# Routing 4096 tokens in three groups of 8, 12 and 12 tiles in place of two of 16

## The chip, the cores and the metric

The kernel runs on one core of one Trainium2 chip. The metric is the device time of one execution in microseconds (us), the median of several runs. The core has five engines with a queue of instructions each: TensorE (PE, with its weight loads as PEld), VectorE (DVE), ScalarE (ACT), GpSimd (POOL) and SyncE (SP). They wait for each other through semaphores; 16 DMA engines move data.

## What is computed

A mixture-of-experts layer with 8 experts, top 2, behind a rotation of the features:

```python
x_rotated = hamilton(q_left_n, hamilton(x_filtered, q_right_conj))   # L0_cond: a fixed map of the 512 features
logits = xf @ gate_w.T                                               # xf: 4096 tokens x 512
scores = softmax(logits); topv, topi = top_k(scores, 2)
gates = topv / sum(topv)
for j in range(2):                                                   # place of each token within its expert
    mask = one_hot(topi[:, j], 8)
    loc_in = cumsum(mask, axis=0) - 1 + offset
    locs.append(loc_in at topi[:, j]); offset = offset + mask.sum(axis=0)
valid = loc < 1024                                                   # capacity
disp[topi * 1024 + loc] += xf * valid
h = relu(disp @ fc1_w.T + fc1_b); eo = h @ fc2_w + fc2_b             # per expert: 1024 x 512 -> 2048 -> 512
out = x + sum over the two choices of eo[topi * 1024 + loc] * gates * valid
```

The rotation is linear in the features and the same for all tokens, so the kernel folds it into a 4x4 matrix `M` per lane and into the gate's weights.

## The kernel before

**Three stages.** First a routing stage, inside `with ExitStack() as rctx` (L166 to L535): it works out, for each of the 8 x 1024 slots, which token fills it (`slot_tok`), and from that the indices for the later gathers and scatters. Then the expert stage (L704 to L1017): TensorE multiplies the gathered tokens with 32 blocks of weights, in a form of Strassen's algorithm with seven products where the plain form has eight (L715, L728), while the other engines gather the next expert's rows, rotate them and add up results. Scatters write the rows back. The order of all instructions is written out by hand: both stages run under `tc.manual_schedule()`, so each engine has its instructions in the order in which the program names them.

**Routing.** The 4096 tokens are 32 tiles of 128, taken in two groups of `TG` = 16 tiles. For each group:

- SP loads four pieces of the transposed input, `xb[g, j]`, 1 MB each (L182). All eight stand at the head of SP's queue, and four loads of weights, 1 MB each, behind them (L107, L113). From the seventh on, a load waits for one that stands eight loads ahead of it, so several are always in flight.
- `logits` (L324): TensorE multiplies each piece with the folded gate weights `Gw`, 8 experts in 32 columns, four column strips side by side.
- `turned` (L338): VectorE transposes the sums from PSUM in 32x32 squares, so that tokens lie on partitions.
- `choose` (L344): VectorE finds the best and second best expert: eleven steps over `TG` x 8 elements, with one `exp` on ScalarE (L357) between them. Its result is wanted by the step at L365. Then a running sum over the tiles of the group in four steps with doubling distance (L371, L373), in bf16 tiles `cnt`, and a carry into the next group's (L377).
- `rank` (L383): two matmuls, with a triangular matrix and with ones, give each token's place within its expert.
- `places` (L395): six VectorE steps split the place into a tile number `hi` and a lane number `lo`.
- `one_hots` (L418): for 8 tiles (`TC`) at a time, VectorE compares `hi` and `lo` with tables of all tile numbers (`tile_no`) and all lanes (`lane`), in fp16: `B` (L428), `W` = `B` times the token's number (L429), and `A` (L433). The last chunk's `A` is made in two parts.
- `tokens` (L440): TensorE multiplies `A` with `W`, 16 small matmuls for each chunk, all into one PSUM tile, `tok_ps`, in which each slot then finds its token.

The order of these calls is the list at L454 to L496: group 0 up to its choice; half of group 1's logits; rank 0; the other half; places 0, the first chunk of one-hots and its tokens; group 1's choice, the totals (L467) and rank 1; group 0's second chunk; then places, both chunks and tokens of group 1. Between them POOL derives from the totals which slots are filled (L484 to L490). The tables `lane` and `tile_no` are made before all this by VectorE (L283 to L296) from counters that POOL writes (L205).

**What follows.** VectorE turns `tok_ps` into `slot_tok` (L501 to L504), after which POOL sends eight gathers of 128 rows (L560). TensorE transposes the first four (L680), VectorE and ScalarE rotate them (L690, L688), and the first matmuls of the expert stage start (L826). VectorE's other outputs of the stage (L505 to L535) are made beside that.

Of the kernel before, what the change touches and what calls it, by code (L numbers as in the profile page):

```python
# [37 lines left out]
P = 128  # L38
# [17 lines left out]

CW = 32
# [7 lines left out]
def kernel(  # L65
# [93 lines left out]
    TG = 16  # L159
    GROUPS = NT // TG  # L160
    TC = 8
# [4 lines left out]
    with ExitStack() as rctx:  # L166
# [12 lines left out]
        for g in range(GROUPS):  # L179
            for j in range(NJ):  # L180
                xb[g, j] = xp.tile([P, QT, TG * CW], F32, tag="xb", name=f"xb{g}_{j}")
                nc.sync.dma_start(xb[g, j], xt[g, j])  # L182
# [20 lines left out]
        def iota(shape, pattern, base, mult, name):  # L203
# [9 lines left out]
            iota([P, P], [[1, P]], 0, 0, "lane0"),  # L213
            iota([P, P], [[-1, P]], P - 1, 0, "lane1"),
# [9 lines left out]
        PAD = 8  # L224
        cnt = [
            [rp.tile([P, PAD + TG + 1, KE], BF16, name=f"cnt{g}_{i}") for i in range(5)]
            for g in range(GROUPS)
        ]
        for g in range(GROUPS):
            for i in range(4):  # L230
                nc.gpsimd.memset(cnt[g][i][:, :PAD], 0.0)

# [46 lines left out]
        lane = rp.tile([P, P, TC, K], F16, name="lane")  # L279
        tile_no = rp.tile([P, E, PT, TC, K], F16, name="tile_no")  # L280
        for k in range(K):
            lane_f = rp.tile([P, P], F32, name=f"lane_f{k}")
            V.tensor_copy(lane_f, lane_i[k])  # L283
            V.tensor_scalar(
                lane[:, :, :, k],
                lane_f.unsqueeze(2).to_broadcast([P, P, TC]),
                -mid,
                None,
                ALU.add,
            )  # L290
            tile_f = rp.tile(TILES, F32, name=f"tile_f{k}")
            V.tensor_copy(tile_f, tile_i[k])
            V.tensor_copy(
                tile_no[:, :, :, :, k].rearrange("p e s t -> p (e s) t"),
                tile_f.rearrange("p e s -> p (e s)").unsqueeze(2).to_broadcast([P, NS, TC]),
            )  # L296
        tile_no = tile_no.rearrange("p e s t k -> p (e s) (t k)")
# [16 lines left out]

        T8 = [P, TG, E]
        revb = rev.unsqueeze(1).to_broadcast(T8)
# [4 lines left out]

        lt_ps = [bank(rps, "lt", g) for g in range(GROUPS)]

        def logits(g, js):  # L324

            for j in js:
                for c in range(QT):
                    nc.tensor.matmul(
                        lt_ps[g][c * CW : (c + 1) * CW],
# [8 lines left out]
        def turned(g):  # L338

            t = gp.tile([P, TG, CW], F32, tag="lt", name=f"lts{g}")  # L340
            V.transpose(t.rearrange("p t w -> p (t w)"), lt_ps[g])
            lg[g] = t[:, :, :E]

        def choose(g):  # L344

            ts = slice(g * TG, (g + 1) * TG)
            mask = cnt[g][0][:, PAD : PAD + TG].rearrange("p t (k e) -> p t k e", k=K)
# [4 lines left out]
            mx = gp.tile([P, TG], F32, tag="mx", name=f"mx{g}")  # L352
            V.tensor_reduce(mx, lg[g], AX.X, ALU.max)
            d = gp.tile(T8, F32, tag="d", name=f"d{g}")
            V.tensor_tensor(d, lg[g], over_e(mx), ALU.subtract)
            ex = gp.tile(T8, F32, tag="ex", name=f"ex{g}")
            nc.scalar.activation(ex, d, AF.Exp)  # L357
            q = gp.tile(T8, F32, tag="q", name=f"q{g}")
            V.scalar_tensor_tensor(q, d, 0.0, revb, ALU.is_equal, ALU.mult)
            for k in range(K):  # L360
# [3 lines left out]
                if k == 0:  # L364
                    V.scalar_tensor_tensor(ex, mask[:, :, 0, :], -2.0, ex, ALU.mult, ALU.add)  # L365
                    V.tensor_reduce(second[:, ts], ex, AX.X, ALU.max)
                    q = gp.tile(T8, F32, tag="q", name=f"q1{g}")
# [4 lines left out]
            for i in range(1, 4):  # L372
# [3 lines left out]
            if g + 1 < GROUPS:  # L376
                V.tensor_tensor(  # L377
                    cnt[g + 1][0][:, PAD - 1], c[4][:, PAD + TG], c[0][:, PAD - 1], ALU.add
                )
# [3 lines left out]
        def rank(g):  # L383
            flat = bank(rps, "rank", g)[:, : TG * KE]
            rank_ps[g] = flat.rearrange("p (t c) -> p t c", c=KE)
            for n, (w, c) in enumerate(((upper, cnt[g][0]), (ones, cnt[g][4]))):
# [3 lines left out]
                    rhs=c[:, PAD : PAD + TG].rearrange("p t c -> p (t c)"),  # L390
                    start=n == 0,
                    stop=n == 1,
                )

        def places(g):  # L395


            each = [P, TG, K]
            r = gp.tile([P, TG, KE], F32, tag="r", name=f"r{g}")
            V.scalar_tensor_tensor(  # L400
                r, rank_ps[g], mid, cnt[g][0][:, PAD : PAD + TG], ALU.subtract, ALU.mult
            )
            loc = gp.tile(each, F32, tag="loc", name=f"loc{g}")
            V.tensor_reduce(loc, r.rearrange("p t (k e) -> p t k e", k=K), AX.X, ALU.add)
            h = gp.tile(each, F32, tag="h", name=f"h{g}")
            V.tensor_scalar(h, loc, 1.0 / P, BIG, ALU.mult, ALU.add)
            V.tensor_scalar(h, h, BIG, None, ALU.subtract)
            lo = gp.tile(each, F16, tag="lo", name=f"lo{g}")
            hi = gp.tile(each, F16, tag="hi", name=f"hi{g}")
            V.scalar_tensor_tensor(  # L410
                hi, rank_first[:, g * TG : (g + 1) * TG], -WIDE, h, ALU.mult, ALU.add
# [6 lines left out]
        def one_hots(g, c, hi, lo, parts=1):  # L418

            hi, lo = (  # L420
                a[:, c * TC : (c + 1) * TC].rearrange("p t k -> p (t k)") for a in (hi, lo)
            )
            tok = tok_no[:, g * TG + c * TC : g * TG + (c + 1) * TC].rearrange("p t k -> p (t k)")
            of_tile = [P, NS, TC * K]
            B = oh.tile(of_tile, F16, tag="B", name=f"B{g}_{c}")
            W[g, c] = oh.tile(of_tile, F16, tag="W", name=f"W{g}_{c}")
            A[g, c] = oh.tile([P, P, TC * K], F16, tag="A", name=f"A{g}_{c}")
            V.tensor_tensor(B, tile_no, hi.unsqueeze(1).to_broadcast(of_tile), ALU.is_equal)  # L428
            V.tensor_tensor(W[g, c], B, tok.unsqueeze(1).to_broadcast(of_tile), ALU.mult)  # L429
# [633 lines left out]
```

## Time and profile before

| what | us |
|---|---|
| median of 3 runs | 1633.86 (1632.6 to 1635.38) |
| the profiled execution | 1635.45 |
| its span | 1633.7 |
| busy: PE / DVE / POOL / ACT | 1584.2 / 922.1 / 893.0 / 283.1 |
| first group's last logits matmul ends | 15.83 |
| VectorE starts group 0 / group 1 (L341) | 15.85 / 26.74 |
| last token matmul ends | 43.53 |
| first row gather starts (L560) | 44.55 |
| first expert matmul starts (L826) | 56.29 |

Times within the execution are counted from the span's start. A line of the timeline or of the chain has a start, a length, the engine, and what it did; "x32" is a number of instructions. A group has a count, the sum of its busy time, the mean of one in ns, and what ended the idle time before it. A line such as L433 is one of the kernel before; after the change, lines lie some 8 to 40 further down.

### The profile page before, as it was taken

What the parts mean: (1) busy time and instruction counts of PE and PEld (TensorE: products, weight loads), DVE (VectorE), ACT (ScalarE), POOL (GpSimd) and SP (SyncE); (2) the same over time, 40 slices, a digit from 0 to 9 for tenths busy, and PEclk for the clock granted to TensorE, in tenths of its full rate; (3) what the DMA queues carried; (4) which work ended last, traced back from release to release, by engine and by line L of the source; (5) the groups of instructions that cost most, each with busy time, mean ns of one, the idle gap of its engine ahead of it and who ended that gap; (6) DMA issues with size and microseconds to landing.
All of it is one profiled execution on the core that took longest, in us unless ns stands there. A gap on an engine that the chain in (4) does not pass through costs nothing.

```text
span 1633.7 us, 14503 instructions
## 1 busy us (share of the span) xinstructions
PE 1584.2 (97%) x5558; PEld 1039.0 (64%) x5558; DVE 922.1 (56%) x1291; ACT 283.1 (17%) x393; POOL 893.0 (55%) x747
## 2 busy tenths in 40 slices
PE   4899999999999999999999999999999999999996
PEld 1456666666666666666666666666666666666665
DVE  7536744476555755567455774447745476454335
ACT  1121211221112211122111221122111221111110
POOL 1576265853568435783367726586266844544304
PEclk8799999999999999999999999999999999999999
DMA  7542103311222112320133210331122211230003
GB/s 311 172 152 72 52 31 113 114 60 52 97 97 72 52 52 110 124 82 1 52 137 108 72 52 7 137 111 63 52 97 75 89 52 52 104 108 31 21 26 102
DMA packets 47998, 137.31 MB, mean 84 GB/s; under 512 B 9334, under 2 KB 9590, under 8 KB 42808
## 3 DMA queue, kind: packets, MB, share of 16 engines
q1 hardware_dynamic: 22800, 75.54, 12.6%
q0 software_dynamic: 20736, 52.32, 9.7%
q10 hardware_dynamic: 4392, 8.52, 1.4%
q8 instruction: 44, 0.72, 0.2%
q14 instruction: 26, 0.21, 0.0%
HBM read 119.77 MB, written 25.23 MB: 89 GB/s over the span
## 4 chain that ended last, share of the span: by engine, by line
PE 93%; issue 2%; DVE 1%; DMA 1%; POOL 1%; ACT 1%; SPq 0%; POOLq 0%; another core or an unknown queue 0%; DVEq 0%; ACTq 0%
PE a L728 26%; PE a L715 26%; PE b L715 20%; PE b L728 19%; PE p L826 2%; DMA xb<-in_xt_dram 1%; POOL rows L560 1%; POOL out_dram L606 0%; DMA rows<-out_dram,slot_tok 0%; PE tok_ps L444 0%; ACT u L759 0%; DMA rows<-in_x_dram,slot_tok 0%; DVE A L433 0%; ACT h L789 0%; PE xps L680 0%
## 5 line engine op out<-in xcount | busy, mean ns | idle before, releaser
L759 ACT ACTIVATE u<-a,b_sb 128x512 f32<-128x512 f32 x186 | 127.7, 686 | 802.4 <-PE a L715 719.2
L637 POOL DMA_INDIRECT xq<-in_xq_dram,quarter x224 | 228.5, 1020 | 62.0 <-issue 60.2
L728 PEld LDWEIGHTS a<-t,hs 128*128 128x128 f32 x1024 | 194.6, 190 | 79.4 <-issue 59.3
L728 PE MATMUL a<-t,hs 128*128 128x256 f32 x1024 | 241.9, 379 | 0.0
L715 PE MATMUL a<-x,s 128*128 128x512 f32 x496 | 233.1, 592 | 0.0
L136 POOL TENSOR_TENSOR s<-w 128x512 f32<-128x512 f32 x31 | 39.3, 1268 | 228.9 <-PE b L715 228.8
L139 POOL TENSOR_TENSOR s<-w,s 128x512 f32<-128x512 f32 x31 | 40.3, 1299 | 202.6 <-PE b L715 202.5
L715 PEld LDWEIGHTS a<-x,s 128*128 128x128 f32 x496 | 94.2, 190 | 65.7 <-issue 59.3
L715 PE MATMUL a<-x,w 128*128 128x512 f32 x248 | 118.4, 600 | 8.1 <-ACT u L759 3.7
L728 PEld LDWEIGHTS b<-w,h 128*128 128x128 f32 x512 | 98.0, 192 | 43.0 <-issue 20.6
L728 PE MATMUL b<-w,h 128*128 128x256 f32 x512 | 122.0, 381 | 2.1 <-DVE acc L989 2.1
L728 PEld LDWEIGHTS a<-t,h 128*128 128x128 f32 x512 | 97.1, 190 | 40.5 <-issue 25.6
L728 PEld LDWEIGHTS a<-w,h 128*128 128x128 f32 x512 | 97.3, 190 | 39.7 <-issue 29.4
L728 PEld LDWEIGHTS b<-t,hs 128*128 128x128 f32 x512 | 97.3, 190 | 39.7 <-issue 25.3
L728 PEld LDWEIGHTS b<-w,hs 128*128 128x128 f32 x512 | 97.3, 190 | 39.2 <-issue 28.9
L728 PE MATMUL a<-t,h 128*128 128x256 f32 x512 | 121.1, 379 | 0.8 <-DVE v L976 0.8
L728 PE MATMUL a<-w,h 128*128 128x256 f32 x512 | 121.0, 379 | 0.0
L728 PE MATMUL b<-t,hs 128*128 128x256 f32 x512 | 120.9, 379 | 0.0
L728 PE MATMUL b<-w,hs 128*128 128x256 f32 x512 | 120.9, 379 | 0.0
L715 PE MATMUL a<-xa,w 128*128 128x512 f32 x248 | 116.6, 592 | 0.8 <-ACT u L759 0.8
L715 PE MATMUL b<-x,s 128*128 128x512 f32 x248 | 116.5, 592 | 0.0
L715 PE MATMUL b<-xb,s 128*128 128x512 f32 x248 | 116.5, 592 | 0.0
(169 smaller groups left out, 2154.0 us busy)
## 6 DMA issues: line engine op xcount, KB each, us to landing
w<-in_w_dram SPq DMA_DIRECT2D x64, 1024.0 KB, 7.8
xb<-in_xt_dram SPq DMA_DIRECT2D x8, 1024.0 KB, 8.6
out_dram<-in_x_dram ACTq DMA_DIRECT2D x1, 8192.0 KB
xq<-in_xq_dram,quarter POOLq DMA_INDIRECT x224
b<-in_b_dram POOLq DMA_DIRECT2D x8, 256.0 KB
c<-choice,slot_cho POOLq DMA_INDIRECT x64
rows<-out_dram,slot_tok POOLq DMA_INDIRECT x64
out_dram<-rows,slot_add POOLq DMA_INDIRECT x64
```

The lines of the kernel that those rows point to most:

```text
L136: lambda: G.tensor_tensor(s[0], w[:, 1, 0], w[:, 1, 1], ALU.add),
L139: lambda: G.tensor_tensor(s[3], w[:, 0, 1], s[1], ALU.subtract),
L560: nc.gpsimd.indirect_dma_start(out=t, out_offset=None, in_=src, in_offset=bass.IndirectOffsetOnAxis(ap=slot_tok[:, s : s + 1], axis=0),)
L637: nc.gpsimd.indirect_dma_start(out=self.xg[half][st][:, q * P : (q + 1) * P], out_offset=None, in_=xq, in_offset=bass.IndirectOffsetOnAxis ...
L715: nc.tensor.matmul(out[:, m], lhsT=factors[0][n][:, c, m * P : (m + 1) * P], rhs=factors[1][n][:, c, :], start=first and c == 0, stop=c == ...
L728: nc.tensor.matmul(out[:, m], lhsT=factors[0][n][:, c, (st0 + m) * P : (st0 + m + 1) * P], rhs=factors[1][n][:, c, :], start=first and m = ...
L759: nc.scalar.activation(to[:, m], a[:, m], func, bias=bias[:, m : m + 1])
L826: nc.tensor.matmul(ps[n][:, m], lhsT=w[:, block, i // 2, i % 2, m * P : (m + 1) * P], rhs=x.of(half, i), start=i == 0, stop=i == NJ - 1,)
```

## The change

- `TG` = 16 and `TC` = 8 give way to `GROUP = (8, 12, 12)`: three groups of different sizes. Twelve loads of `xt` (four of 0.5 MB, eight of 0.75 MB) take the place of eight of 1 MB. Tiles are made for 12 (`TM`) and cut to the group's size, so that group 0's pieces land in rows of 384 elements of which 256 are filled.
- One-hots are made for a whole group at once: three sets in place of four, the last with `A` in three parts.
- The tables `lane` and `tile_no` grow from 8 to 12 tiles and are written by ScalarE: `lane` ahead of group 0's `exp` on its queue, `tile_no` behind it. The lane counters are made twice as large with the middle already taken off, and ScalarE halves them.
- Group 0 needs three running-sum steps (`SUMS`), the others four. After 12 tiles the 16 long sum already covers the carried row, so the carry and the totals are then a copy and one matmul (`all_before`).
- The order of the calls is a new list, for three groups.

The rest of `choose`, `rank`, `places` and `tokens` changes only in sizes and names.

```diff
+GROUP = (8, 12, 12)
...
-    TG = 16
-    GROUPS = NT // TG
-    TC = 8
+    GROUPS = len(GROUP)
+    FROM = [sum(GROUP[:g]) for g in range(GROUPS)]
+    TM = max(GROUP)
...
-                xb[g, j] = xp.tile([P, QT, TG * CW], F32, tag="xb", name=f"xb{g}_{j}")
-                nc.sync.dma_start(xb[g, j], xt[g, j])
+                size = QT * GROUP[g] * CW
+                at = P * (NJ * QT * CW * FROM[g] + j * size)
+                xb[g, j] = xp.tile([P, QT, TM * CW], F32, tag="xb", name=f"xb{g}_{j}")[
+                    :, :, : GROUP[g] * CW
+                ]
+                nc.sync.dma_start(
+                    xb[g, j],
+                    xt[at : at + P * size].rearrange("(p c f) -> p c f", p=P, c=QT),
+                )
...
+        SUMS = [(n - 1).bit_length() for n in GROUP]
...
             V.tensor_copy(lane_f, lane_i[k])
-            V.tensor_scalar(
+            nc.scalar.activation(
                 lane[:, :, :, k],
-                lane_f.unsqueeze(2).to_broadcast([P, P, TC]),
-                -mid,
-                None,
-                ALU.add,
-            )
-            tile_f = rp.tile(TILES, F32, name=f"tile_f{k}")
-            V.tensor_copy(tile_f, tile_i[k])
-            V.tensor_copy(
-                tile_no[:, :, :, :, k].rearrange("p e s t -> p (e s) t"),
-                tile_f.rearrange("p e s -> p (e s)").unsqueeze(2).to_broadcast([P, NS, TC]),
-            )
+                lane_f.unsqueeze(2).to_broadcast([P, P, TM]),
+                AF.Copy,
+                scale=0.5,
+            )
+            tile_f.append(rp.tile([P, NS], F32, name=f"tile_f{k}"))
+            V.tensor_copy(tile_f[k], tile_i[k].rearrange("p e s -> p (e s)"))
+
+        def tile_tables():
+            for k in range(K):
+                nc.scalar.copy(
+                    tile_no[:, :, k::K], tile_f[k].unsqueeze(2).to_broadcast([P, NS, TM])
+                )
...
-            for i in range(1, 4):
+            for i in range(1, SUMS[g]):
                 V.tensor_tensor(
                     c[i + 1][:, PAD:], c[i][:, PAD:], c[i][:, PAD - 2**i : -(2**i)], ALU.add
                 )
             if g + 1 < GROUPS:
-                V.tensor_tensor(
-                    cnt[g + 1][0][:, PAD - 1], c[4][:, PAD + TG], c[0][:, PAD - 1], ALU.add
-                )
+                carry = cnt[g + 1][0][:, PAD - 1]
+                if len(all_before(g)) == 1:
+                    V.tensor_copy(carry, all_before(g)[0])
+                else:
+                    V.tensor_tensor(carry, *all_before(g), ALU.add)
+
+        def all_before(g):
+            n = GROUP[g]
+            own, before = cnt[g][SUMS[g]][:, PAD + n], cnt[g][0][:, PAD - 1]
+            return [own] if 2 ** SUMS[g] > n else [own, before]
...
-        def one_hots(g, c, hi, lo, parts=1):
+        def one_hots(g, hi, lo, parts=1):
+            hi, lo = (a.rearrange("p t k -> p (t k)") for a in (hi, lo))
+            n = GROUP[g] * K
...
+            B = oh.tile([P, NS, TM * K], F16, tag="B", name=f"B{g}")[:, :, :n]
+            W[g] = oh.tile([P, NS, TM * K], F16, tag="W", name=f"W{g}")[:, :, :n]
+            A[g] = oh.tile([P, P, TM * K], F16, tag="A", name=f"A{g}")[:, :, :n]
...
         logits(0, range(NJ))
         turned(0)
         choose(0)
-        logits(last, range(NJ // 2))
+        tile_tables()
+        logits(1, range(HJ))
         rank(0)
-        logits(last, range(NJ // 2, NJ))
+        logits(1, range(HJ, NJ))
         at = places(0)
-        one_hots(0, 0, *at)
-        tokens(0, 0)
-        turned(last)
-        choose(last)
+        one_hots(0, *at)
+        turned(1)
+        choose(1)
+        logits(2, range(HJ))
+        tokens(0)
+        rank(1)
+        logits(2, range(HJ, NJ))
+        at = places(1)
+        turned(2)
+        choose(2)
         tot_ps = bank(rps, "rank", NT)[:, :KE]
...
-        rank(last)
-        one_hots(0, 1, *at)
-        tokens(0, 1)
+        rank(2)
+        one_hots(1, *at)
+        tokens(1)
...
         at = places(last)
-        one_hots(last, 0, *at)
-        tokens(last, 0)
-        one_hots(last, 1, *at, parts=2)
-        tokens(last, 1)
+        one_hots(last, *at, parts=3)
+        tokens(last)
```

## The prediction

> **What bounds the kernel now.** I read the page first, then the chain of work that ended last.
>
> ```profile
> span 1633.7 us, 14503 instructions
> PE 1584.2 (97%) x5558; PEld 1039.0 (64%) x5558; DVE 922.1 (56%) x1291; ACT 283.1 (17%) x393; POOL 893.0 (55%) x747
> ```
>
> TensorE is busy 97% of the span, and the diff touches none of that work: only the routing before it. The order of instructions of the built kernel says so too: from the first row gather on, every engine has the same instructions as before. So the change can move only the moment at which `slot_tok` (L504) lets the gathers start; all that follows moves along. The start of the chain:
>
> ```profile
> 2.59 11.65 DMA xb<-in_xt_dram
> 14.28 1.54 PE lt L328 x8
> 15.85 0.73 DVE lts L341
> ...
> 38.15 1.14 DVE A L433
> 39.30 0.05 issue
> 39.34 4.20 PE tok_ps L444 x32
> ...
> 44.55 1.25 POOL rows L560
> ...
> 56.29 12.18 PE p L826 x24
> ```
>
> Three links (start, length, what): the first four 1 MB loads up to 15.85 (their matmuls end there), VectorE without a break to 39.30, 32 small matmuls to 43.55. Call the first moment T0. At most 44 us, 2.7% of the span, are in play. The durations that I scale, from the groups with shapes kept apart (count | busy us, mean ns):
>
> ```profile
> L433 DVE TENSOR_TENSOR A<-lane,lo 128x2048 f16<-128x2048 f16 x3 | 3.7, 1229 | 0.0
> L428 DVE TENSOR_TENSOR B<-tile_no,hi 128x1024 f16<-128x1024 f16 x4 | 2.7, 684 | 0.0
> L433 DVE TENSOR_TENSOR A<-lane,lo 128x1024 f16<-128x1024 f16 x2 | 1.3, 685 | 0.0
> L404 DVE TENSOR_REDUCE loc<-r 128x32 f32<-128x256 f32 x2 | 0.8, 420 | 0.1
> L359 DVE SCALAR_TENSOR_TENSOR q<-d,rev 128x128 f32<-128x128 f32 x2 | 0.6, 294 | 0.1
> ```
>
> 16-bit work: (1229-684)/1024 = 0.53 ns per element; fp32: (420-294)/128 = 1.0, I take 1.04; the rest, some 0.15 us, is paid per instruction whatever the size. The third row, parts of 8 out of 16 neighbours, costs no more than whole rows (second row), so I price group 0's rows (16 out of 24) the same.
>
> **T0, the first group.** It shrinks from 4 MB to 2 MB. Before, TensorE's waits for loads ended at 6.88, 9.29, 11.80, 14.28: 2.5 us per MB. Two MB would have landed at 9.3. But group 0 now goes into a tile of 12: 1 KB runs in place of 8 KB. The DMA view in windows has the nearest rows; the first is of 8 KB runs, the second is nearly all `w2`, with 2 KB runs:
>
> ```profile
> DMA packets 1107, 8.02 MB, mean 422 GB/s; under 512 B 128, under 2 KB 128, under 8 KB 128
> DMA packets 372, 0.80 MB, mean 401 GB/s; under 512 B 7, under 2 KB 7, under 8 KB 363
> ```
>
> A 2 KB run takes 82 to 86 ns of one of 16 engines (401 and 383 GB/s, two windows) where 422 GB/s makes it 78: 4 to 8 ns per run. A 1 KB run is then 39+7 = 46 ns, and 128 runs per engine cost 0.9 us more (bounds: 0, and 1.1). Against that, loads of half the size should land with less lead between engines, -0.4. So 9.3+0.9-0.4 = 9.8; the last four matmul pairs at half width take 1.0 (1.93 halved) and T0 = 10.85. Bounds 9.5 (no run cost, fast clock) and 11.4. That is 5.0 us earlier than 15.85.
>
> A rule speaks against smaller loads: the Trainium skill, "DMA: Bandwidth & Descriptors", section "Bandwidth", wants at least 1 MiB per DMA for 75% of peak, and gives 2.0 us + bytes/436e3 for each. By it, taken one after the other, four loads of 0.5 MB are 12.8 us. The trace's 1 MB loads, which the rule puts at 4.4, land every 2.5, as several are in flight; twelve loads keep that. I take the row.
>
> **VectorE's chain.** Group 0: before 15.85 to 26.82 = 10.97. With 8 tiles: transpose -0.27, eleven choice steps of 64 elements less -0.73, one of four running sums gone -0.40 and three halved -0.20, `r` and `loc` -0.27, small steps and rank -0.17; B, W, A keep their size. 8.93.
> Group 1 up to `hi`/`lo`: before 26.82 to 32.63 (transpose, choice, sums) 5.81 and 35.19 to 36.83 (places) 1.64. For 12 tiles -0.64 and -0.16. Its places now come at once after its sums, so they pay the trip to the rank matmul, 0.44 in group 0 (22.25 to 22.69). 7.09, at T0+16.0.
> Group 2's choice and sums: 5.17. Then B, W, A of group 1: before 2.56, B and W +0.27 each, A +0.54: 3.64. Places of group 2: 1.48. B and W of group 2: before 1.32, +0.54: 1.86. First third of A: 0.65.
> Sum: T0+16.0+5.17+3.64+1.48+1.86+0.65 = T0+28.8, plus a wait w.
>
> The wait: group 2's transpose needs its last two logits chunks, and TensorE's queue holds them behind `tokens(0)` and `rank(1)`, which waits for group 1's sums at T0+14.1 = 24.95. Rank 0.45, then two chunks of 384 columns: 0.8 each at the fast clock, 1.45 at the slow one (1.06 and 1.93 of the before trace at 512): ready at 26.9 to 28.2. VectorE asks at 26.85. w = 0.1 to 1.4; I take 0.7, since the clock before read 0.50 up to 25.6. Data are no later: the last MB landed at 24.3, +0.5 to 0.9. `tokens(0)` (16 matmuls, 2.19) stand behind group 2's first two chunks, which land at about 21, so they end at 24.2, just clear of 24.95.
>
> **The tail on TensorE.** Before, 32 token matmuls run after 39.34; now 24 after the first third of A. Two windows of 1 us (PE busy and count first, near the end the granted clock):
>
> ```profile
> 27.00:28.00 1.00, 1.00 (x9) 1.00 (x10) 0.93 (x3) 0.00 (x0) 0.00 (x0) 1.00 1.10 412
> 41.00:42.00 1.00, 1.00 (x11) 0.92 (x10) 0.89 (x2) 0.00 (x0) 0.00 (x0) 0.50 0.00 0
> ```
>
> Clock 1.00 or 0.50, about the same number of matmuls: their pace, 4.20/32 = 0.131 us, is not the clock's, so a warmer TensorE buys nothing here (the Trainium skill, "TensorE: Matmul & The Clock Gate", "Part 1: The HAM clock gate", would halve it). 24 x 0.131 = 3.15; VectorE's last third comes 1.2 after the first, so TensorE ends last. 24 of group 1 need 3.15 between T0+25.5 and T0+28.8: just clear.
>
> End: 10.85+28.8+0.7+3.15 = 43.5, against 43.55. The 5.0 us that T0 wins are spent: a third pass of transpose, choice, sums and places (every fixed cost again), the rank trip, the wait.
>
> **What is hidden.** VectorE's tables go (L284 0.63 and L293 0.34 apart in start, twice: 1.94): it is through at 8.4 instead of 10.3, both before T0; worth 0 (0.8 at T0 = 9.5). ScalarE takes them, ahead of group 0's `exp`. Its row for 128x1024 from SBUF is 1.06; 128x1536 is then 1.06+512x0.83 = 1.48 at the per-element figure of the Trainium skill, "ScalarE: Activation LUTs", section "What ACT_TABLE_LOAD costs". Two, overlapping, from 6.6 end at 9.5; the load of the exp table behind them, 1.28 in the trace, ends at 10.8. The same section puts a switch at 2.66, a drain included; in the trace `rt` starts 0.02 after its load, so I take 1.28 (with 2.66: 12.15). `exp` is wanted at T0+1.0 = 11.9, its result at T0+1.8: hidden either way. The `tile_no` copies (about 0.8 each) end near 13.8; B wants them at T0+6.4. Two bounds for ScalarE's 2-byte writes in 4-byte steps, which no row shows: as any, or half the rate (rival C). POOL: three more memsets of 0.15, done before 5; its seven steps after `total` (33.18 to 36.98) still end 5 us early. SP: four more issues of 0.43; weights land under 1 us later, about 34.5, wanted at 55. The first gather also waits for TensorE now, but for a token matmul that is over by then.
>
> **Rivals.**
> A, faster: runs of 1 KB cost nothing, the chunks run at the fast clock and the 0.41 stall at 20.7 (inside the 10.97) goes: T0 -1.35, w -0.7, -0.41: end at 41.1, 1631.4. For it: matmuls at 16.8 were already fast. Against: 2 KB runs do show a price. Another 0.8 anywhere takes it over 0.2%.
> B, slower: the 1 KB runs of group 0 (SP's four first loads) are slow. Everything hangs on T0, so each ns per run costs 128 ns. Over 0.2% (3.3 us) begins at 46+26 = 72 ns; at half rate (78) T0 is 4.1 later, 1638. For it: no row has such runs on an empty queue. Against: 2 KB runs take 83.
> C: ScalarE writes its tables at half rate: 6.6+2x2.75 = 12.1, table 13.4, `exp` done 13.7, 1.0 later than VectorE wants it: 1635.
> That the change doesn't do what it says: the order of instructions shows three groups, so no.
>
> **Numbers.** The profiled execution took 1635.45 (span 1633.7); the sum takes 0.1 from it. The median of the runs is 1633.86; the same shift gives 1633.8. Three runs lie 1632.6 to 1635.38 apart, so about 0.2% (3.3 us) is what can be told from no change. Chances: forecast 0.50 (of it 0.03 each way outside 0.2%), A 0.20 (0.15 of it past 0.2%, with another term too large), B 0.17, C 0.13 (0.04 past it, if the wait doubles). Faster 0.18, same 0.58, slower 0.24. The range leaves out the far ends of A and B: 1630.8 to 1637.6.
>
> **What would show it.** Right: transpose of group 0 near 10.9, group 2's near 27.5 with a wait on TensorE, tokens ending near 43.5, the first gather within 1.5 us of 44.55. T0 past 12: the runs are dear. VectorE waiting for ScalarE at the first `ex` step (L384): C. No wait at group 2's transpose and a gather before 42: A. A change after the first gather would refute the whole reading.

## The result, and the profile after the change

| | before | after |
|---|---|---|
| median of 22 runs each, us | 1633.83 (1632.05 to 1637.03) | 1636.33 (1634.96 to 1638.94) |
| ratio, 95% interval | | 1.0015 (1.0009 to 1.0022) |
| the profiled execution, us (its span) | 1635.45 (1633.7) | 1634.96 (1633.2) |
| VectorE starts group 0 (T0) | 15.85 | 11.56 |
| last token matmul ends | 43.54 | 44.57 |
| first row gather starts | 44.55 | 46.25 |
| first expert matmul (p) starts | 56.29 | 57.74 |

The change costs 2.5 us (1.5 to 3.6 by the interval). On a second chip, where the kernel before takes 1622.98, the ratio was 1.0009 (1.0000 to 1.0018). The time lies inside the predicted range, but the forecast was no change (-0.1 us), and it is slower. The two profiled executions can't show this by their spans, which differ by less than single executions do; the stretch up to the first gather can.

The page of after, first lines: TensorE's share and its work are what they were.

```profile
span 1633.2 us, 14603 instructions
PE 1585.9 (97%) x5591; PEld 1040.2 (64%) x5591; DVE 914.7 (56%) x1307; ACT 289.0 (18%) x398; POOL 898.1 (55%) x750
```

The chain of work that ended last, after, first 58 us (start, length, what):

```profile
3.19 7.17 DMA xb<-in_xt_dram
10.41 1.13 PE lt L340 x8
11.56 0.46 DVE lts L353
...
20.41 0.51 DVE lts L353
...
25.64 0.32 PE rank L416
25.96 2.76 PE lt L340 x16
28.75 0.59 DVE lts L353
...
40.85 0.61 DVE A L463
41.52 3.05 PE tok_ps L474 x24
...
45.05 0.23 DVE slot_tok L543
...
45.87 0.37 DVE picked L560
46.25 1.21 POOL rows L599
```

The links are the predicted ones: the loads to 11.56, VectorE, a wait at group 2's transpose (25.96 to 28.75, TensorE in the chain for 2.76 us), a tail of 24 matmuls. New is the end: the chain lets the gather hang on `picked` (L560), a reciprocal whose result it doesn't read. `slot_tok` had ended at 45.28, so the gather starts 0.97 after it, where before it started 0.29 after `slot_tok`; before, from the chain and from GpSimd's timeline:

```profile
44.03 0.23 DVE slot_tok L504
44.55 1.25 POOL L560 DMA_INDIRECT rows<-in_x_dram,slot_tok  x1 [7.57 <-DVE tokf L505]
```

Groups of after, shapes kept apart (count | busy us, mean ns of one | idle before):

```profile
L294 ACT ACTIVATE lane<-lane_f 128x1536 f16<-128x1536 f32 x2 | 3.7, 1904 | 1.8 <-DVE lane_f L293 1.8
L456 DVE TENSOR_TENSOR B<-tile_no,hi 128x1536 f16<-128x1536 f16 x2 | 1.9, 954 | 0.0
L463 DVE TENSOR_TENSOR A<-lane,lo 128x3072 f16<-128x3072 f16 x1 | 1.8, 1790 | 0.0
L433 DVE TENSOR_REDUCE loc<-r 128x24 f32<-128x192 f32 x2 | 0.7, 354 | 0.1
```

VectorE's rows are as the before rows scaled: 684+512x0.53 = 955 for B (954), 1229+1024x0.53 = 1772 for A (1790), 420-64x1.04 = 353 for `loc` (354). Only ScalarE's writes were dearer: 1.90 instead of 1.48. The 0.83 ns per element that the prediction took from the Trainium skill ("ScalarE: Activation LUTs", "What ACT_TABLE_LOAD costs") does not hold for this write, and the measurement decides.

### The profile page after: what moved, and what is told of

Its sections match the earlier page's. It is cut to its first block, busy times and chain, and to the rows that moved or that the text cites. A ratio compares the mean times of both kernels' runs of the same rounds, so it can differ in the third digit from the quotient of the medians.

```text
span 1633.2 us, 14603 instructions
## 1 busy us (share of the span) xinstructions
PE 1585.9 (97%) x5591; PEld 1040.2 (64%) x5591; DVE 914.7 (56%) x1307; ACT 289.0 (18%) x398; POOL 898.1 (55%) x750
## 4 chain that ended last, share of the span: by engine, by line
PE 93%; issue 2%; DVE 2%; ACT 1%; POOL 1%; DMA 1%; DVEq 0%; SPq 0%; POOLq 0%; another core or an unknown queue 0%; ACTq 0%
PE a L767 26%; PE a L754 26%; PE b L754 20%; PE b L767 18%; PE p L865 2%; POOL rows L599 1%; DMA xb<-in_xt_dram 0%; ACT h L828 0%; POOL out_dram L645 0%; ACT u L798 0%; ACT xa L727 0%; PE lt L340 0%; ACT h L798 0%; DMA rows<-out_dram,slot_tok 0%; DMA rows<-in_x_dram,slot_tok 0%
## 5 line engine op out<-in xcount | busy, mean ns | idle before, releaser
L754 PE MATMUL b<-xa,w 128*128 128x512 f32 x248 | 116.5, 592 | 0.0
## 6 DMA issues: line engine op xcount, KB each, us to landing
xb<-in_xt_dram SPq DMA_DIRECT2D x8, 768.0 KB, 10.2
```

Of the source, the lines that this page charges most:

```text
L754: nc.tensor.matmul(out[:, m], lhsT=factors[0][n][:, c, m * P : (m + 1) * P], rhs=factors[1][n][:, c, :], start=first and c == 0, stop=c == ...
```

## Experiments

Lines carry numbers of the profile of each kernel. "Gap" is from the end of `slot_tok` to the first gather. Each ratio is taken against runs of the kernel before on the same chip. e1, e2, e3 and e4_tables ran on one where that kernel takes 1633.54; c1, e5, e6 and b2 on a second (1622.98); e4_again, e7, b1 and e8 on a third (1623.18). Microseconds within the profiled execution, then the ratio of the times:

| kernel | T0 | wait, last group's transpose | tokens end | gap | gather | p | ratio to before (95%) |
|---|---|---|---|---|---|---|---|
| before | 15.85 | 0 | 43.54 | 0.29 | 44.55 | 56.29 | 1 |
| after | 11.56 | 1.26 | 44.57 | 0.97 | 46.25 | 57.74 | 1.0015 (1.0009 to 1.0022) |
| c1_after | 11.75 | 1.27 | 44.77 | 0.97 | 46.45 | 58.06 | 1.0009 (1.0000 to 1.0018) |
| e1_exact | 10.01 | 1.27 | 43.26 | 0.97 | 44.94 | 56.64 | 1.0006 (0.9998 to 1.0014) |
| e2_addr | 11.88 | 1.26 | 45.45 | 0.29 | 46.46 | 58.15 | 1.0008 (1.0001 to 1.0016) |
| e3_order | 11.79 | 0 | 43.97 | 0.96 | 45.65 | 57.17 | 1.0006 (0.9996 to 1.0015) |
| e4_tables | 11.54 | 0 | 43.33 | 0.97 | 45.00 | 56.38 | 1.0009 (1.0001 to 1.0017) |
| e4_again | 11.93 | 1.26 | 45.07 | 0.96 | 46.74 | 58.14 | 1.0012 (1.0002 to 1.0021) |
| e5_all | 10.18 | 0 | 41.89 | 0.29 | 42.89 | 54.37 | 0.9992 (0.9983 to 1.0001) |
| e6_picked | 12.16 | 1.27 | 45.16 | 0.97 | 46.83 | 58.35 | 1.0012 (1.0003 to 1.0021) |
| e7_two | 14.82 | 1.49 | 44.19 | 0.95 | 45.85 | 57.41 | 1.0010 (1.0001 to 1.0019) |
| b1_pad | 15.46 | 0 | 42.87 | 0.96 | 44.53 | 56.06 | 1.0002 (0.9993 to 1.0011) |
| b2_delay | 15.86 | 0 | 43.13 | 0.29 | 47.57 | 59.33 | 1.0018 (1.0009 to 1.0027) |
| e8_best | 10.33 | 0 | 41.83 | 0.29 | 42.84 | 54.32 | 0.9990 (0.9980 to 0.9999) |

A ratio's interval is about 1.4 us wide each way, as large as most of the terms. So the terms are read from the profiles, and the ratios only for the sum of several.

**1. Tiles of group 0's own size.**

```diff
-                xb[g, j] = xp.tile([P, QT, TM * CW], F32, tag="xb", name=f"xb{g}_{j}")[
-                    :, :, : GROUP[g] * CW
-                ]
+                pool = xp if GROUP[g] == TM else xs
+                xb[g, j] = pool.tile([P, QT, GROUP[g] * CW], F32, tag="xb", name=f"xb{g}_{j}")
```

> Group 0's four loads go into tiles of their own size, 8 token tiles wide, so that each partition's part lands as one 4 KB run in place of four 1 KB runs; the data, their order and everything behind them stay. My theory: the changed kernel lost 1.1 us at its first transpose against the 10.4 or so that half the data should need, and the short runs are the reason (a 0.5 MB load landed every 1.47 us, where 422 GB/s makes it 1.24: four times 0.23 is 0.9). Then group 0's transpose starts at 10.5 to 10.7 instead of 11.56, TensorE's token matmuls end at 43.5 to 43.7 instead of 44.57, and the time falls by 0.9 us to about 1635.4. Rival 1: it is not the length of the runs but the size of a load (0.5 MB, with the latency of each one less well covered); then the transpose stays at 11.4 to 11.6 and the time too. Rival 2: the run length matters, but the last logits chunks of group 2 then come no earlier, because all 8 MB land at the same time; the wait at group 2's transpose grows by what group 0 won, and the token matmuls still end near 44.5.

T0 fell to 10.01, more than expected: 1.55 us less, and rival 1 falls. TensorE ran its four chunks from 6.15, when its weights `Gw` were ready, without a wait for data, so T0 is now set by TensorE at 0.95 a chunk; all four loads had landed by 9.0 (in e5 and e8 the fourth is seen to land at 9.03 and 9.19). With 1 KB runs the fourth landed at 10.39 to 11.02 in seven profiles, 10.65 in the mean: 1.5 us later, or 12 ns for each of the 128 runs per engine. The windows show where (time, busy time of PE, PEld, DVE, ACT, POOL, granted clock, DMA share, GB/s); after first, then exact tiles:

```profile
2.00:4.00 2.00, 0.00 (x0) 0.00 (x0) 1.30 (x5) 1.96 (x6) 2.00 (x15) 1.00 0.64 150
4.00:6.00 2.00, 0.00 (x0) 0.00 (x0) 1.25 (x8) 0.56 (x2) 0.61 (x5) 1.00 1.09 372
6.00:7.00 1.00, 0.99 (x8) 0.20 (x8) 0.96 (x10) 0.67 (x1) 0.00 (x0) 1.00 0.93 211
```

```profile
2.00:4.00 2.00, 0.00 (x0) 0.00 (x0) 1.16 (x5) 1.82 (x6) 2.00 (x15) 1.00 0.91 243
4.00:6.00 2.00, 0.00 (x0) 0.00 (x0) 1.25 (x7) 0.71 (x2) 0.58 (x4) 1.00 1.01 410
6.00:7.00 1.00, 0.85 (x8) 0.40 (x12) 0.96 (x9) 0.53 (x1) 0.00 (x0) 1.00 1.04 422
```

The last number of each row is what moved: a slower start (150 against 243), a lower rate in flow (372 against 410), and a dip at 6 to 7 us (211 against 422, with the engines shown 93% busy). SP also took longer to issue a load (median of the twelve 0.55 against 0.43 us).

The 12 ns are not the price of a run. In the single packets of these traces, from 4 to 9 us, a 1 KB run of after takes a median of 46 ns on its engine and a 4 KB run of e1 159, or 39.75 per KB: 6 ns more per run, 0.8 us for 128. The rest, some 0.7 of the 1.5, goes to the start and the dip. In the dip of after five packets, begun at 6.08 to 6.20, took 0.69 to 1.00 us each, and e1 has no packet like that after 4 us. Why they stood so long is open.

Rival 2 held in a small part: `tokens(0)` now stood in the way of rank(1), and VectorE waited 0.34 at `r`, so that the tokens end 1.31 earlier, not 1.55.

**2. Addresses.** In the changed kernel a part of the one-hots that TensorE reads, W of group 1, lies at the addresses of the first row buffer; so the gather that fills it waits for TensorE too. The edit moves W and A below it:

```diff
-        gp = rctx.enter_context(tc.tile_pool(name="gp", bufs=2))
         oh = rctx.enter_context(tc.tile_pool(name="oh", bufs=2))
+        gp = rctx.enter_context(tc.tile_pool(name="gp", bufs=2))
+        bp = rctx.enter_context(tc.tile_pool(name="bp", bufs=2))
+        dp = rctx.enter_context(tc.tile_pool(name="dp", bufs=1))
...
-            B = oh.tile([P, NS, TM * K], F16, tag="B", name=f"B{g}")[:, :, :n]
+            B = bp.tile([P, NS, TM * K], F16, tag="B", name=f"B{g}")[:, :, :n]
```

(the scratch tiles `prod` and `gprod` go to `dp`.)

> Only addresses in SBUF move: the one-hots A and W, which TensorE reads, go below the address of the first row buffer of the gathers, and the tiles that only VectorE and ScalarE touch (B, the choice's scratch, two scratch tiles of the prologue) go above it. The first gather then carries no wait for TensorE, only the one for slot_tok, as in the kernel before. My theory: in the changed kernel the first gather started 0.97 us after the end of slot_tok (45.28 to 46.25) where the kernel before took 0.29, and the second wait on GpSimd's queue, an instruction of its own, is what costs the 0.68 us. Then the gap is 0.3 us here, x's first product (p) starts at about 57.05 instead of 57.74, and the time falls by 0.7 to about 1635.6. Rival: the gap comes from VectorE's reciprocal beside it (the trace names that as the releaser) or is a scatter of GpSimd's start; then the gap stays near 1.0 and the time does not move.

The gap went from 0.97 to 0.29. In this execution group 2's second load landed at 22.99, against 22.16 in after; `tokens(0)` and rank(1) stand behind it on TensorE, and VectorE waited 0.69 at `r`. So the tokens ended 0.88 later and p did not start earlier (58.15): the expected 0.7 is there in the gap, and the later data of this one execution hide it in the sum.

**3. Is it the wait, or the reciprocal beside it?** Two more kernels. In the first, what makes `picked` stands ahead of VectorE's wait for the tokens:

```diff
+        den = rp.tile([P, NT], F32, name="den")
+        V.tensor_scalar(den, second, 1.0, None, ALU.add)
+        V.reciprocal(picked[:, :, 0], den)
...
         tok = rp.tile([P, K, NS], F32, name="tok")
         V.tensor_tensor(tok[:, 0], tok_ps[:, 0, :], has0, ALU.mult)
```

> In the changed kernel, the four VectorE instructions that make the table of choices (den, its reciprocal and two copies), which stood behind slot_tok, stand ahead of VectorE's wait for the token matmuls, where it idles 2.0 us. The first gather keeps both its waits. It tells two causes of the late gather apart (0.97 us after slot_tok's end with the wait for TensorE, 0.29 without). Theory 1: the wait for TensorE is an instruction of its own and costs 0.68 by itself; then the gap stays at 0.9 to 1.0. Theory 2: the extra instruction only makes the gather late enough to run into VectorE's next instructions, up to the reciprocal, at whose end it started in each of the five profiles that have the wait, and GpSimd's start waits for them; then with the reciprocal gone the gap is 0.3 to 0.6 and the time falls by some 0.4 to 0.6.

The second is the kernel before, with padding that moves its last A into the row buffer's addresses:

```diff
+        pad = rp.tile([P, 1408], F32, name="pad")
+        V.memset(pad[:, :1], 0.0)
         xb = {}
```

> The kernel before, with an unused tile of 5.5 KB per partition added to the routing's SBUF, which moves the last one-hots A up into the addresses of the first row buffer; nothing else changes but one small memset. The first gather then carries a second wait, for the token matmuls, as in the changed kernel. It is the converse of the run in which the addresses were parted. My theory: the gap from slot_tok's end to the first gather goes from 0.29 to 0.97, and the time up by 0.7, to a ratio of about 1.0004. Rival: in the kernel before, with the same instructions beside it, the second wait costs nothing; the gap stays 0.29.

The end of `slot_tok` in the chain, for e2, e6 and b1 (after's is shown above), and then GpSimd's timeline, the first gather, in after, e2, e6 and b1 in turn (start, length, what, and in brackets the idle time before it and what the trace takes for its releaser):

```profile
45.94 0.23 DVE slot_tok L545
```

```profile
45.64 0.22 DVE slot_tok L549
```

```profile
43.34 0.23 DVE slot_tok L506
```

```profile
46.25 1.21 POOL L599 DMA_INDIRECT rows<-in_x_dram,slot_tok  x1 [6.09 <-DVE picked L560]
```

```profile
46.46 1.25 POOL L601 DMA_INDIRECT rows<-in_x_dram,slot_tok  x1 [5.41 <-DVE tokf L546]
```

```profile
46.83 1.21 POOL L599 DMA_INDIRECT rows<-in_x_dram,slot_tok  x1 [6.09 <-DVE slot_add L551]
```

```profile
44.53 1.21 POOL L562 DMA_INDIRECT rows<-in_x_dram,slot_tok  x1 [8.24 <-DVE picked L523]
```

With the reciprocal gone (e6) the gap is still 0.97, and the trace merely names the instruction that now ends last ahead of the gather. With the second wait alone put into the kernel before (b1), the gap goes from 0.29 to 0.96. So theory 1 holds: the wait for TensorE, long fulfilled (the tokens ended 1.7 us ahead of the gather in after), costs 0.68. In the built programs of after, e6 and b1 an instruction of its own on GpSimd's queue takes the wait for `slot_tok`, and the gather behind it waits for the last token matmul; in before and e2 the gather waits for `slot_tok` itself, and the page of e2 counts 14602 instructions where after has 14603. The Trainium skill, "Perfetto Trace Analysis", section "Identifying Dependency Chains", says that an instruction that waits for several engines may get such an instruction put in front; these programs agree, and the 0.68 is from the runs. The ratio of b1, 1.0002, can't resolve 0.7 us.

**4. Order on TensorE.**

```diff
         logits(2, range(HJ))
         tokens(0)
+        logits(2, [HJ])
         rank(1)
-        logits(2, range(HJ, NJ))
+        logits(2, range(HJ + 1, NJ))
```

> TensorE's queue gets one change of order: group 2's third logits chunk ahead of group 1's rank matmuls instead of behind them, so that only one chunk lies between the rank and group 2's transpose. My theory: the 1.26 us that VectorE waits at group 2's transpose are the two chunks of 1.4 us each at TensorE's slow clock, run after rank(1); with one of them moved into the 1.4 us that TensorE waits for group 1's sums the wait goes to 0 to 0.2, the token matmuls end at 43.4 to 43.6 instead of 44.57 and the time falls by 1.1 to 1.2, to about 1635.2. Rival 1: the third chunk of data has not landed by then, the rank matmuls are held up behind it, and group 1's places start up to 1 us later: the sum stays. Rival 2: VectorE's wait goes but GpSimd's or TensorE's later work (token matmuls of group 1) takes its place: end of the token matmuls within 0.3 us of 44.57.

The wait at group 2's transpose went from 1.26 to 0, and rival 1 took back 0.56 of it: behind `tokens(0)` the third chunk ran from 24.82 to 26.19 at the slow clock, and rank(1) after it. From T0 to the tail it is 29.12 us instead of 29.96. e5 also puts `tokens(0)`, which nobody needs then, behind the last chunk.

**5. Tables on VectorE again**, run twice.

```diff
-            nc.scalar.activation(
+            V.tensor_scalar(
                 lane[:, :, :, k],
                 lane_f.unsqueeze(2).to_broadcast([P, P, TM]),
-                AF.Copy,
-                scale=0.5,
+                0.5,
+                None,
+                ALU.mult,
             )
```

(and `tile_no` by `V.tensor_copy`, without `tile_tables`.)

> The lane and tile tables are written by VectorE again, 12 tiles wide, at the end of its prologue; ScalarE writes none. My theory: ScalarE's tables were hidden in the changed kernel and so were VectorE's before; VectorE's prologue ends near 7.65 + 2.9 = 10.6, still ahead of the first transpose at 11.56, and nothing moves: the token matmuls end within 0.2 us of 44.57, the time within 0.5 us. What could move: nothing of group 0 waits for ScalarE's tables or its table load any more. Rival: ScalarE's writes or its exp, late behind the tables and the table load, hold group 0's choice up or slow VectorE beside them; then the time from the first transpose to the second (8.85 us) falls by 0.3 or more here, and the end with it.

> The run with the tables on VectorE once more, unaltered: in its first profile group 2's last two chunks ran at the fast clock (1.50 us together, granted clock 1.00 up to 30) and the wait at group 2's transpose was gone, where the changed kernel had 2.79 and a wait of 1.26 in both of its profiles. My theory: TensorE's clock goes up and down in steps whose phase differs from execution to execution, and it was chance; then this profile is as likely to show 2.8 us for the two chunks and a wait of 1.2 again. Rival: with ScalarE's tables gone the clock is always up there; then the two chunks take 1.5 again, the wait is 0, and the token matmuls end near 43.3.

The first run refuted "nothing moves": the tokens ended 1.24 earlier. But T0 was the same to 0.02 and group 0 took 8.96 instead of 8.85 (transpose to transpose in the chain), so neither side of the theory had moved. What had moved is TensorE's clock. Windows of after, then of the first run with tables on VectorE (the granted clock is the third number from the end; where it misleads is said below):

```profile
23.00:26.00 3.00, 2.56 (x24) 2.10 (x26) 2.28 (x11) 0.00 (x0) 0.00 (x0) 0.69 1.02 419
26.00:29.00 3.00, 2.68 (x16) 0.48 (x16) 1.60 (x7) 0.00 (x0) 0.00 (x0) 0.50 0.99 380
```

```profile
23.00:26.00 3.00, 2.49 (x26) 2.13 (x26) 2.37 (x10) 0.00 (x0) 0.00 (x0) 1.00 1.00 412
26.00:29.00 3.00, 1.40 (x16) 0.32 (x16) 2.71 (x11) 0.28 (x1) 0.00 (x0) 1.00 1.03 393
```

The same 16 matmuls: 2.68 us at 0.50, 1.40 at 1.00. The second run of the very same kernel had the slow clock and the wait back (TensorE's timeline):

```profile
26.37 2.79 PE L338 MATMUL lt<-xb,Gw 128*32 128x384 f32 x16
```

So it was chance: of the seven profiles with group 2's last two chunks behind rank(1), six have 2.79 and a wait of 1.26 to 1.27, one has 1.50 and none. The column of the granted clock is not enough to see it. c1 reads 1.00 over the slow chunks too:

```profile
26.07 2.79 PE L340 MATMUL lt<-xb,Gw 128*32 128x384 f32 x16
```

```profile
27.00:27.50 0.50, 0.50 (x8) 0.15 (x4) 0.43 (x4) 0.00 (x0) 0.00 (x0) 1.00 0.96 377
27.50:28.00 0.50, 0.50 (x10) 0.05 (x4) 0.15 (x2) 0.00 (x0) 0.00 (x0) 1.00 0.97 365
```

The first clock record of each trace is a rise, and the column reads 1.00 up to it whatever the chunks take: in c1 it comes at 28.8, in e1 at 59.7 and in e2 at 61.6, and until then each chunk of group 1 or 2 took the slow 1.50 to 1.51 (two in a row 2.79). So in these three the clock had not yet risen, and in after, e4_again and e6 it had risen and fallen again. In after the fast clock lasted from 17.3 (the chunk at 16.17 took 1.38, between the slow 1.51 and the fast 0.85) to 24.1, 6.8 us; in the first run of e4 from 20.0 to 30.2, 10.2 us. That agrees with the Trainium skill, "TensorE: Matmul & The Clock Gate", "Part 1: The HAM clock gate", by which the clock goes up after a busy window and down after an idle one, the window being about 3.4 us long and running free of the kernel: two windows and three. The tables are hidden, as predicted.

**6. What a microsecond at the gather is worth.** The kernel before, with eight more VectorE instructions on scratch data ahead of `slot_tok`:

```diff
         V.tensor_tensor(tok[:, 1], tok_ps[:, 1, :], not0, ALU.mult)
+        for _ in range(8):
+            V.tensor_scalar(sign_x, sign_x, 1.0, None, ALU.add)
```

> The kernel before, with eight extra VectorE instructions of 512 elements (they add 1 to a scratch tile that nothing reads) between the token matmuls and slot_tok. It measures what a microsecond at the first gather is worth at the end. My theory is one to one: the profile gives their length, some 3 to 6 us from the rows of 1.04 ns per element at the most, the first gather comes as much later and so does the end, within the noise of 1 us; time 1637 to 1639. Rival: later work has slack (weights and factor sums that are late, TensorE's cold start), and only part of it, under two thirds, reaches the end.

The gather came 4.44 after the tokens' end instead of 1.01, 3.43 later. The ratio, 1.0018, is 2.9 us (1.5 to 4.4). One to one lies within that, and so does the rival's "under two thirds" (up to 2.3). The spans of the profiles decide. In the eight of the second and third chip, p starts between 54.32 (e8) and 59.33 (b2), and from p to the end it is 1564.5 to 1566.1 us in all of them; a straight line through the eight gives 1.1 us of span for each us of p (95% interval 0.85 to 1.4). In the other six (before, after, e1, e2, e3 and e4_tables) that stretch scatters more, 1573.2 to 1577.4, which is why the spans of before and after, 1633.7 and 1633.2, hide what their first 58 us show.

**7. Two groups of 16, with the rest of the change.**

```diff
-GROUP = (8, 12, 12)
+GROUP = (16, 16)
...
-        one_hots(0, *at)
         turned(1)
         choose(1)
...
-        one_hots(last, *at, parts=3)
+        one_hots(last, *at, parts=4)
```

(with `rank(1)`, `one_hots(0)` and `tokens(0)` behind `choose(1)`, and no third group.)

> The change without its three groups: two groups of 16 tiles, as before, with the rest of the change kept (one-hots of a whole group at once, the last in four parts; tables on ScalarE; the first gather's wait for TensorE). It says what the rest is worth alone. My theory: T0 is that of the kernel before, 15.5 to 15.9; VectorE saves three one-hot instructions of group 0 and two of group 1 at 0.15 each, and loses 0.55 because group 1's B and W are done whole before the first part of A; TensorE's tail is 32 x 0.131 = 4.2 as before; so the token matmuls end at 43.1 to 43.7 (before 43.54), the gather comes at 44.9 to 45.4 (before 44.55) because of its second wait, and the time is 0.4 to 0.9 above the kernel before: about equal within the noise. Rival: whole-group one-hots are worth more or less than their instruction count (16-bit rows that are longer run faster); then the stretch from T0 to the first part of A differs from 23.5 by over 0.5.

From T0 to the first part of A it is 25.15 us, 1.49 of them a wait at group 1's transpose; without it 23.66, against 23.45 before. So whole-group one-hots are worth nearly nothing. The wait comes from e7's own order of calls: half of group 0's one-hots used to fill the time in which group 1's last load came in, and in e7 all of them stand behind `choose(1)`. I had not expected that wait, and so the tokens end at 44.19, outside what was expected, although T0, at 14.82, is 1.0 earlier than in before (its last load landed 0.6 earlier, and its last chunk ran at the fast clock, 1.06 us). With the gap of 0.95 the gather comes at 45.85. In this order the rest of the change is no gain without the three groups; another order was not tried.

**8. Everything repaired.** Own-size tiles, the addresses, and TensorE's queue with `tokens(0)` last:

```diff
-        logits(2, range(HJ))
-        tokens(0)
+        logits(2, range(HJ + 1))
         rank(1)
-        logits(2, range(HJ, NJ))
+        logits(2, range(HJ + 1, NJ))
+        tokens(0)
```

> Three edits together: group 0's loads in tiles of their own size; the addresses that spare the first gather its wait for TensorE; and a queue on TensorE in which group 2's third chunk stands ahead of group 1's rank matmuls, and group 0's token matmuls (2.1 us) behind group 2's last chunk, since in the run with exact tiles they held up the rank by 0.3. My theory, in which all that counts is the moment of the first gather: T0 9.98 as with exact tiles (before that TensorE is bound by its own four chunks from 6.15 on), the wait at group 2's transpose 0 to 0.3 in place of 1.2, the token matmuls' end 42.1 to 42.4, the gather 1.0 after it at 43.1 to 43.4 (the kernel before: 44.55), the time 1.2 to 1.4 us below the kernel before: about 1632.3. Rival: the gathers and weights then collide in the DMA queues, or x's first stage waits for something else (w1's sums on GpSimd, the weights), so that the stage's first product (p) does not start before 56.0, and the time stays at that of the kernel before.

> The three edits together once more (exact tiles for group 0, addresses that spare the gather its wait, TensorE's queue with the token matmuls of group 0 last), and the last group's A in six parts in place of three, so that TensorE's tail starts after 4 columns' worth of tiles less. My theory: the first part takes 0.42 in place of 0.61 us; TensorE's tail of 24 x 0.131 = 3.1 still ends last, since VectorE needs 5 x 0.42 = 2.1 behind the first part; so the token matmuls end 0.2 earlier than the 41.9 of the three edits, at 41.7, the first gather comes at 42.7 (before 44.55), and the time is 1.5 to 2.0 below the kernel before, a ratio of 0.9988 to 0.9991. Rival: the earlier gather is not passed on (x's first stage took 12.8 us in the last run where it took 12.2 before, with TensorE at the slow clock), and the time is within 1 us of the kernel before.

With the changed kernel beside them on the same chip (control):

> The changed kernel once more, unaltered, so that the others of this call stand beside it on the same chip, and so that a second profile of it shows which of its waits are the same in each execution. In the run with VectorE's tables nothing was to move, but group 2's two chunks took 1.50 us together in place of 2.79 and the wait of 1.26 at group 2's transpose was gone. My theory: that has nothing to do with the tables; which clock TensorE has for these two chunks differs from execution to execution. Then this profile can show either 2.8 or 1.5 for them, with a wait of 1.2 or 0; T0 (the start of the first transpose) is 11.5 to 11.9 and the gap from slot_tok's end to the first gather 0.97 in any case. Rival: the tables on ScalarE fix it, and the two chunks take 2.8 here as well, as they did in the three other runs. Time about 1635.5 to 1636.5.

In e5, which ran beside c1, the tokens end 2.9 earlier than in c1 and the gather comes 3.6 earlier; the times are 1621.47 against 1624.59, 3.1 less. Against the kernel before, e5 is 1.5 us faster with an interval that just takes in 1, e8 1.6 us faster, 0.9990 (0.9980 to 0.9999): the only version whose interval lies below 1, and it does so barely. In e8, A in six parts brought its 0.2 (first part to tail 0.35 instead of 0.61), but T0 came 0.15 later in that execution. The chain of work in e8:

```profile
35.09 0.28 DVE r L431
...
38.38 0.35 DVE A L465
38.77 3.06 PE tok_ps L476 x24
...
42.84 1.25 POOL rows L601
```

In e8 the gather is 1.71 ahead of before's, p (54.32) 1.97 ahead, and the time 1.6. c1 showed the slow chunks, the wait of 1.27 and the gap of 0.97 again, as in after.

## Why the prediction was wrong, step by step

The plan of the path held. Three terms of its sum failed: T0, the wait at group 2's transpose, and the gather's second wait, which was put at nothing.

- **What bounds the kernel; where the change can act.** Right. TensorE's work in the expert stage is untouched, and the time moves with the first gather and p about one to one (experiment 6).
- **T0 = 10.85: failed; 11.56 in after, 11.54 to 12.16 in all.** The price of a run was right: "39+7 = 46 ns" is what the packets took. What failed is the step from there to "0.9 us more", as if the queue ran full from its start: the slow start and the dip come on top, and the short runs cost 1.3 in after (10.41 against 9.11, where the fourth load with whole runs landed in the mean of e5 and e8) and 1.5 in the mean of seven. "Against that, loads of half the size should land with less lead between engines, -0.4" has nothing behind it: that 9.11 lies among the times of the second 1 MB load, 9.29 in the profile that I used and 8.72 to 9.03 in three others; against the 9.3-0.4 of the sum it is 0.2 late. From the landing to T0 it was 1.15 instead of 1.05. Together 0.4+0.2+0.1 = 0.7.
- **The rule on small loads** (12.8 us for the four, taken one after another): the trace's side was right, with the four landed at 9.03 and 9.19 in e5 and e8. The formula stands in that page's section "Anatomy of one DMA — SWDGE (gpsimd) path", not under "Bandwidth", and was fitted to transfers that GpSimd issues; here SP issues them. Half-size loads with whole runs were not slower; the length of the runs counts, not the size of the load.
- **VectorE, T0+28.8 without the wait:** right; it was 28.65. Group 0 took 8.85 of the 8.93, the rows scaled as told.
- **The wait w, 0.7 from 0.1 to 1.4: inside, at the wrong end.** 1.26, two chunks at the slow clock. I took the middle because "the clock before read 0.50 up to 25.6"; in after it fell at 24.1, ahead of the chunks at 25.89. Six profiles of seven show the slow end: to take the middle of two states that don't mix was the mistake.
- **TensorE's tail, 24 x 0.131 = 3.15:** right, 3.05. It did not depend on the clock: 16 token matmuls took 2.10 at a granted clock of 1.00 (e4_tables, at 23.04) and 2.09 at 0.50 (e5, at 25.93). The prediction's reading held, not the halving that it names from the page.
- **The first gather: failed.** "The first gather also waits for TensorE now, but for a token matmul that is over by then", costed at nothing. A fulfilled wait costs 0.68 here: with it the program has one more instruction ahead of the gather (e2, e6 and b1 show the cost from three sides). "Within 1.5 us of 44.55" was broken by 0.2.
- **What is hidden:** right. ScalarE's tables took 1.90 each instead of 1.48, the table load ended at 11.31 instead of 10.8, and `exp` was wanted at 12.56. VectorE's tables were worth nothing in either place (e4).
- **The rivals.** A is out: the runs cost, the clock was slow, and the 0.41 stall stayed (VectorE idle for 0.52 ahead of L373 in before, for 0.52 ahead of L400 in after). B named the right place, group 0's short runs, but put the price at 72 ns per run and more; it is 46, or 39+12 = 51 with the start and the dip spread over the runs. C is out, with its full half rate (2.75) not reached. None of the three held: the slower end is the sum of the three terms above.

The sum: T0 +0.71, the wait +0.56, VectorE and the tail -0.2, the gather's second wait +0.68, which is the 1.7 by which after's gather (46.25) misses the 44.5 that the prediction meant. That is what one profile of each shows. The medians say 2.5 (and 1.5 on the second chip). Before's gather was late in the profile that I had: without what was added to them, b1 and b2 have it at 43.85 and 44.14, so that the mean of three is 44.2, of after and c1 46.35: 2.2 apart. So the profiles account for 1.7 to 2.2 of it; how much of the difference between 1.5, 2.2 and 2.5 is more than scatter stays open.

## What to carry to other kernels

A smaller piece cut from a tile made for a larger one breaks its rows: ask for the length of the contiguous run in the destination, not the bytes of the load. When tile sizes change, addresses change with them; look at which buffers of the next stage now lie on what another engine reads, because even a wait that was over by then cost 0.68 us here, in front of a transfer on the critical path. And where a value has two states, such as a clock, forecast one of them and put the other in the range: the middle is a value that neither gives.

## What was not expected of the hardware

- A second, fulfilled wait ahead of an indirect gather on GpSimd: 0.96 to 0.97 instead of 0.29 us from the end of `slot_tok` to its start, in nine profiles with it against five without (0.95 in one of the nine).
- 1 KB runs on a fresh queue: 46 ns each where a KB of a 4 KB run takes 39.75, and on top a slow start and a dip to 211 GB/s at 6 to 7 us, in which five packets took up to 1.00 us; 12 ns per run in all. Whether making the descriptors has a part in it (SP's issues took 0.55 instead of 0.43 us) was not tried.
- TensorE at half clock in the routing: the same two chunks took 2.79 or 1.50 us in two executions of one kernel, and the column of the granted clock read 1.00 in c1, e1 and e2 while they took 2.79.
- ScalarE writing 1536 16-bit elements at every second place: 1.90 us, 1.24 ns per element.
